# Tokens times Wq^T Wk as seven products of half-size blocks, from the second batch on

## The chip, the cores and the metric

The kernel runs on one core of a Trainium2 chip. The metric is the device time of one execution in microseconds. TensorE is called PE here (its weight loads PEld), VectorE DVE, ScalarE ACT, GpSimd POOL, and SyncE, whose queue issues most DMAs, SP.

## The reference

Eight batches of 256 tokens x 1024 features (x) and 256 context rows x 1024 (ctx_4096) go through a gated cross attention and a gated feed-forward block. Cut to what matters:

```python
xn = _layernorm(x)
Q = einsum('btx,dx->btd', xn, Wq) + bq          # 1024 x 1024
K = einsum('bpx,dx->bpd', ctx, Wk) + bk
attn = softmax(einsum('btd,bpd->btp', Q, K) / sqrt(1024))
x = x + tanh(g_xattn) * einsum('btp,bpd->btd', attn, ctx)
# feed-forward, 1024 -> 2752 -> 1024; each linear layer quantises its input rows
# and its weight rows to 8-bit steps (max-abs / 127) before the product
h = silu(qlinear(xn2, w_gate)) * qlinear(xn2, w_up)
x = x + tanh(g_ffn) * qlinear(h, w_down)
```

All inputs and the output are float32.

## The kernel before

The kernel has three parts. The first (to about 107 us) forms the map M = Wq^T Wk, 1024 x 1024 in f32, kept in SBUF as `mt` [128, 8, 1024], by seven products of half-size blocks. The bias of the queries becomes a column vector `u_col`. The second part, the attention half (about 107 to 455 us), runs over the eight batches. The third is the feed-forward part in bf16 (about 460 us to the end), whose weights stream through a ring of four buffers `wring` (tag `wp`, 8 KB per partition each), loaded by SP from the quantised copies in DRAM.

In the attention half the tokens of a batch lie transposed in `xT` [128, 8 feature chunks, 256 tokens], and `H` [128, 8, 256] is M^T applied to them plus `u_col`. `queries_product(j)` makes chunk j of H: eight matmuls of a 128 x 128 block of `mt` with 256 columns of `xT`, summed in a PSUM bank (tags g and s), and one ACT operation that adds the bias and writes H. `scores` multiplies H with the transposed features `fT` into two PSUM banks, one for each tile of 128 tokens; the eight matmuls of a tile read chunks 0 to 7 of H in order.

The order of every engine is the order of the program (`manual_schedule`). For batch b the program is: `softmax_stage(b)` (scores of tile 0, transposes of two quarters of the next batch's tokens into xT, half of the scores of tile 1, the other two quarters, the rest), then blocks 0 to 7 of the *next* batch's H through `queries_between(j)`, with work of this batch between them: `attend` after blocks 1 and 2 (attention times features), `residual` on DVE after each, statistics and normalisation of tokens on DVE, transposes of the next features (`features_transposed`, copied by ACT) after blocks 2 to 5, and `steps` on DVE (normalise, row maximum, scale to quantisation steps) for the two token tiles. `store_steps` rounds them on ACT and stores them.

Between all this `prepare()` advances the quantisation of the feed-forward weights by one piece: SP loads `raw`, DVE takes the row maximum (L126), POOL scales (L220 for w_gate and w_up, L232 for w_down), ACT rounds to bf16 (L257, L245), and SP transposes and stores. Load, DVE and POOL, ACT, and store belong to different pieces in one call: piece i is loaded, piece i-2 gets its maximum and scaling, piece i-3 is rounded. Four `raw` buffers go round. In batches 0 to 4 `queries_between` calls it from block 2 on, in batches 5 and 6 from block 1 on.

In batch 6 the first four weight buffers of the feed-forward part are loaded (`load_weights` at blocks 1, 3, 5 and 7).

Of the kernel before, what the change touches and what calls it, by code (L numbers as in the profile page):

```python
# [9 lines left out]
F32 = mybir.dt.float32  # L10
BF16 = mybir.dt.bfloat16
AF = mybir.ActivationFunctionType
ALU = mybir.AluOpType
# [4 lines left out]
P = 128  # L18
# [9 lines left out]
def gated_xattn_ffn_kernel(  # L28
# [26 lines left out]
    nc = tc.nc  # L55
    B, S, D = x.shape
# [3 lines left out]
    NTT = S // P  # L60
# [5 lines left out]
    HB = 512  # L66
# [8 lines left out]
    small = ctx.enter_context(tc.tile_pool(name="small", bufs=2))  # L75
# [29 lines left out]
    def store_as_rows(dst, cols, tag, pool):  # L105

        n = cols.shape[1]
        pt = bank(tag)
        nc.tensor.transpose(pt[:n, :P], cols, ident)
        rows = pool.tile([n, P], F32, name="rows", tag="rows", bufs=2)  # L110
        nc.scalar.copy(rows, pt[:n, :P])
        nc.gpsimd.dma_start(out=dst, in_=rows)
# [50 lines left out]
    def bank(tag):  # L163

        return psum.tile([P, HB], F32, name="ps_" + tag, tag=tag)
# [8 lines left out]
    if True:  # L174
        wraw = keep_scope.enter_context(tc.tile_pool(name="wraw", bufs=4, side=right))
        wkeep = keep_scope.enter_context(tc.tile_pool(name="wkeep", bufs=1, side=right))
        mt = wkeep.tile([P, KC, D], F32, name="mt")
        u_col = wkeep.tile([P, KC], F32, name="u_col")
# [88 lines left out]
        def prepare_keep(i):  # L267
            src, kind, part, r = pieces[i]
            if i in turned:
                slot = r % 2 if kind == "wgT" or rows_of(r) < P else r % 2 + 2  # L270
                nc.sync.dma_start(out=w_dram[r // 2][:, slot], in_=turned.pop(i))

        def prepare(n=1):
            for _ in range(n):
                i = step[0]
                if 0 <= i - 5 < len(pieces):
                    prepare_keep(i - 5)
                if i < len(pieces):
                    prepare_load(i)
                if 0 <= i - 3 < len(pieces):  # L280
                    prepare_store(i - 3)
                if 0 <= i - 2 < len(pieces):
                    prepare_scale(i - 2)
                step[0] += 1
# [9 lines left out]
        KH = KC // 2  # L294
# [3 lines left out]
        xT = f_right.tile([P, KC, NTT * P], F32, name="xT", tag="xT")  # L298
# [98 lines left out]
        for k in range(KH):  # L397
            pm = bank("g" if k < 2 else "tr")
# [43 lines left out]
        def transposes(src, blocks):  # L442
            pt = bank("tr").rearrange("p (i t) -> p i t", t=P)
            for i, k in enumerate(blocks):
                nc.tensor.transpose(pt[:, i, :], src[:, k * P : (k + 1) * P], ident)  # L445
            return pt
# [17 lines left out]
        def quarter_transposed(dst, src, g, copy):  # L464

            t, ks = g // 2, range(g % 2 * 4, g % 2 * 4 + 4)
            pt = transposes(src[t], ks)
            copy(dst[:, ks.start : ks.stop, t * P : (t + 1) * P], pt)  # L468
# [12 lines left out]
        stats = Rows()  # L481
# [41 lines left out]
        wring = ctx.enter_context(tc.tile_pool(name="wring", bufs=4, reuse_waits="tile"))  # L523
        weights, loads = [], [p for b in range(B) for p in range(NPR)]

        def load_weights():
# [11 lines left out]
        f_left = work_scope.enter_context(  # L538
            tc.tile_pool(name="f_left", bufs=1, reuse_waits="tile")
        )  # L540
        H = work.tile([P, KC, NTT * P], F32, name="H", bufs=1)
        fT = work.tile([P, KC, L], F32, name="fT", bufs=1)

        def queries_product(j):

            ph = bank("s" if j in (2, 4, 6) else "g")[:, : NTT * P]
            for k in range(KC):
                nc.tensor.matmul(  # L548
                    ph, lhsT=mt[:, k, j * P : (j + 1) * P], rhs=xT[:, k, :],
                    start=(k == 0), stop=(k == KC - 1),  # L550
                )
            nc.scalar.activation(H[:, j, :], ph, AF.Identity, bias=u_col[:, j : j + 1])

        def features_transposed(b, g, copy):
            quarter_transposed(fT, [f_tiles[b][:, l, :] for l in range(NLT)], g, copy)
# [8 lines left out]
        def scores(ps, t, js):  # L564
            for j in js:
                nc.tensor.matmul(  # L566
                    ps[:, :L], lhsT=H[:, j, t * P : (t + 1) * P], rhs=fT[:, j, :],
                    start=(j == 0), stop=(j == KC - 1),
# [51 lines left out]
        def steps(i, xr, stats):  # L620
            normalise(xr, xr, stats, i % NTT)
            scaled(i, xr, nc.vector)
            return xr
# [21 lines left out]
        stats = Rows()  # L645
        for j in range(KC):
            queries_product(j)
            prepare()
            if j == 2:
                for t in range(NTT):  # L650
                    stats.sums(t, xn[t])
            if j == 3:
                stats.root()
                stats.inverse()
            if j in (4, 5):
                normalise(xn[j - 4], xn[j - 4], stats, j - 4)
            if j == 3:
                load_features(1, f_left)
            if j in (2, 3, 4, 5):
                features_transposed(0, j - 2, nc.scalar.copy)  # L660

        def softmax_stage(b, xn):

            nxt = b + 1 < B
            pss = [bank("s") for _ in range(NTT)]
            scores(pss[0], 0, range(KC))
            if nxt:
                quarter_transposed(xT, xn, 0, nc.scalar.copy)
                quarter_transposed(xT, xn, 1, nc.scalar.copy)
            nums = [numerators(pss[0], shift(pss[0], cq[b][:, 0:1]))]  # L670
            scores(pss[1], 1, range(KC // 2))
            if nxt:
                quarter_transposed(xT, xn, 2, nc.scalar.copy)
                quarter_transposed(xT, xn, 3, nc.scalar.copy)
                prepare()
            scores(pss[1], 1, range(KC // 2, KC))
            nums.append(numerators(pss[1], shift(pss[1], cq[b][:, 1:2])))
            return nums

        def queries_between(j):  # L680
            queries_product(j)
            if j > (0 if b > B - 4 else 1):
                prepare()
            if b == B - 2 and j % 2:
                load_weights()

        waiting = None
        for b in range(B - 1):
            nxt = b + 2 < B
            nums = softmax_stage(b, xn)  # L690
            tokens_bias(b + 1, xn, scratch)
            if waiting:
                store_steps(*waiting)
            queries_between(0)
            xr = load_tokens(b, "xr")
            if nxt:
                xn = load_tokens(b + 2, "xn")
            pT = numerators_transposed(nums[0][0])
            prepare()
            queries_between(1)  # L700
            pas = attend(b, pT)
            pT = numerators_transposed(nums[1][0])
            residual(b * NTT, pas, xr[0], nums[0][1])
            nc.gpsimd.dma_start(out=x2_dram[b * NTT], in_=xr[0])
            if nxt:
                stats = Rows()
                for t in range(NTT):
                    stats.sums(t, xn[t])
                stats.root()
            prepare()  # L710
            queries_between(2)
            if nxt:
                stats.inverse()
                for t in range(NTT):
                    normalise(xn[t], xn[t], stats, t)
            features_transposed(b + 1, 0, nc.scalar.copy)
            pas = attend(b, pT)
            residual(b * NTT + 1, pas, xr[1], nums[1][1])
            nc.gpsimd.dma_start(out=x2_dram[b * NTT + 1], in_=xr[1])
            stats = Rows()  # L720
            stats.sums(0, xr[0])
            prepare()
            queries_between(3)
            stats.sums(1, xr[1])
            stats.root()
            if nxt:
                load_features(b + 2, (f_right, f_left)[b % 2])
            features_transposed(b + 1, 1, nc.scalar.copy)
            queries_between(4)
            stats.inverse()  # L730
            y = steps(b * NTT, xr[0], stats)
            features_transposed(b + 1, 2, nc.scalar.copy)
            queries_between(5)
            store_steps(b * NTT, y)
            features_transposed(b + 1, 3, nc.scalar.copy)
            if b == B - 2:
                store_as_rows(sx_dram[: b * NTT, :], sx_all[:, : b * NTT], "tr", work)
            queries_between(6)
            y = steps(b * NTT + 1, xr[1], stats)
            queries_between(7)  # L740
            waiting = (b * NTT + 1, y)
        assert step[0] >= len(pieces) + 3 and not turned
        keep_scope.close()
# [242 lines left out]
    first = {"xq": tokens_in, "sx": sx01[:, 0:1, :], "h": [], "tag": "s"}  # L986
# [6 lines left out]
    xr = load_tokens(B - 1, "xr")  # L993
# [11 lines left out]
    stats = Rows()  # L1005
# [6 lines left out]
    y = {}  # L1012
# [161 lines left out]
    b = B - 1  # L1174
# [52 lines left out]
    t, half = key = ALL[3]  # L1227
    for i in range(2):
        cols = slice(i * HB // 2, (i + 1) * HB // 2)
# [45 lines left out]
```

## Time and profile before

| | |
|---|---|
| time, median of 3 runs | 917.39 us (917.38 to 917.77) |
| profiled execution: span from first to last instruction | 914.9 us |
| its instructions | 14767 |
| granted TensorE clock, mean | 0.999 |
| PE busy | 906.3 us (99%) |
| DVE, ACT, POOL busy | 658.3, 466.6, 329.2 us |
| matmul groups of L548 (queries): busy | 144.6 us (bank tag g), 86.9 us (tag s) |
| matmul groups of L566 (scores), L595 (attend) | 58.9, 57.6 us |

The profile gives the span of one execution; the time of a run is measured around it, 2.5 us more at the median. In a line of the groups stand line, engine, operation, tiles and shape, count, busy time, mean duration of one, and the idle time just before with what ended it. In a line of the timeline stand start, duration, engine, line, operation, tiles and count, and in brackets the idle time before it and its releaser. One f32 matmul leaves two records on PE and two weight loads on PEld.

### The profile page before, as it was taken

Reading aid. Unit: us, or ns where it says so; the run is one execution under the profiler, and the core shown is the slowest. Engines: PE = TensorE matmul, PEld = TensorE weight load, DVE = VectorE, ACT = ScalarE, POOL = GpSimd, SP = SyncE. Lnnn points to the kernel's source line nnn. Section 1 sums busy time; section 2 is a strip of 40 time slices with the busy share of each in tenths; the row PEclk is TensorE's granted clock in tenths of the full one; section 3 lists DMA queues with packets and bytes.
Section 4 is the critical chain, followed back from the end, with each engine's and each line's share of the span. In section 5 each row is a group of like instructions: output and inputs, shape, how many; then the busy total and the mean of one; then the engine's idle time right before and its main releaser. Section 6 shows DMA issues by size and latency. Waiting matters only on the chain.

```text
span 914.9 us, 14767 instructions
## 1 busy us (share of the span) xinstructions
PE 906.3 (99%) x5379; PEld 681.3 (74%) x5394; DVE 658.3 (72%) x1328; ACT 466.6 (51%) x812; POOL 329.2 (36%) x444
## 2 busy tenths in 40 slices
PE   9999999999999999999999999999999999999997
PEld 5444588888887878787878886858778586876854
DVE  5888845958585858685678888676676766767677
ACT  0123334454545444544438688466484755748450
POOL 0034211212121212121112367639194582928621
PEclk9999999999999999999999999999999999999999
DMA  9359988789888889997779995977959597784821
GB/s 329 131 147 329 288 192 243 223 229 259 244 245 248 239 221 256 252 259 225 245 230 307 355 346 161 331 205 272 308 187 335 165 320 241 249 321 140 288 69 69
DMA packets 137848, 221.98 MB, mean 243 GB/s; under 512 B 92056, under 2 KB 93360, under 8 KB 127536
## 3 DMA queue, kind: packets, MB, share of 16 engines
q1 hardware_dynamic: 125872, 189.82, 69.0%
q0 software_dynamic: 6720, 22.56, 6.6%
q10 hardware_dynamic: 5184, 8.66, 2.6%
q8 instruction: 42, 0.69, 0.3%
q14 instruction: 30, 0.25, 0.1%
HBM read 167.52 MB, written 32.26 MB: 218 GB/s over the span
## 4 chain that ended last, share of the span: by engine, by line
PE 94%; DVE 4%; DMA 1%; issue 0%; ACT 0%; DVEq 0%; SPq 0%
PE ps_g L788 17%; PE ps_tr L788 16%; PE ps_g L548 14%; PE ps_s L548 8%; PE ps_s L948 7%; PE ps_s L566 6%; PE ps_a L595 5%; PE ps_a L948 5%; PE ps_s L342 4%; PE ps_tr L445 3%; PE ps_a L342 3%; PE ps_tr L342 2%; PE ps_g L342 2%; PE ps_g L1182 1%; DMA xn<-in_x_dram 1%; PE ps_tr L1182 1%
## 5 line engine op out<-in xcount | busy, mean ns | idle before, releaser
L788 PEld LDWEIGHTS <-wp 128*128 128x128 bf16 x2752 | 269.2, 98 | 33.0 <-issue 0.6
L788 PE MATMUL ps_g<-xqb,wp 128*128 128x256 bf16 x1408 | 168.1, 273 | 0.0
L788 PE MATMUL ps_tr<-xqb,wp 128*128 128x256 bf16 x1344 | 161.1, 273 | 0.0
L220 POOL TENSOR_SCALAR raw<-raw,inv 128x1024 f32<-128x1024 f32 (+1 forms) x44 | 56.3, 1280 | 247.5 <-DVE inv L122 140.1
L548 PE MATMUL ps_g<-xT,mt 128*128 128x256 f32 x640 | 144.6, 379 | 0.2 <-ACT xT L468 0.2
L548 PEld LDWEIGHTS ps_g<-xT,mt 128*128 128x128 f32 x640 | 120.3, 190 | 19.1 <-issue 3.3
L800 ACT ACTIVATE g<-g,swg 128x256 f32<-128x256 f32 (+1 forms) x176 | 79.6, 498 | 55.1 <-DVE g L798 54.9
L798 DVE TENSOR_TENSOR g<-ps_g,sx 128x512 f32<-128x512 f32 x88 | 60.7, 690 | 54.3 <-PE ps_g L788 54.1
L813 DVE SCALAR_TENSOR_TENSOR h<-ps_tr,swu,g 128x256 f32<-128x256 f32 x168 | 74.0, 480 | 35.8 <-PE ps_tr L788 25.5
L548 PE MATMUL ps_s<-xT,mt 128*128 128x256 f32 x384 | 86.9, 379 | 0.0
L257 ACT ACTIVATE rq<-raw,nmagic 128x1024 bf16<-128x1024 f32 (+1 forms) x44 | 50.6, 1149 | 59.4 <-POOL raw L220 52.7
L976 POOL TENSOR_TENSOR c<-c,swd_bc 128x512 f32<-128x512 f32 x26 | 33.0, 1271 | 130.6 <-issue 122.0
L548 PEld LDWEIGHTS ps_s<-xT,mt 128*128 128x128 f32 x384 | 71.2, 190 | 8.7
L948 PEld LDWEIGHTS <-gs 128*128 128x128 bf16 x385 | 37.6, 98 | 42.3
L821 ACT ACTIVATE ps_a<-h 128x512 f32<-128x512 f32 (+2 forms) x77 | 43.0, 558 | 51.3 <-DVE h L813 51.3
L566 PE MATMUL ps_s<-fT,H 128*128 128x256 f32 x256 | 58.9, 379 | 0.0
L927 POOL TENSOR_TENSOR gs<-hq 128x256 bf16<-128x256 bf16 x77 | 51.4, 668 | 18.3 <-ACT hq L887 18.0
L595 PE MATMUL ps_a<-fn,pT 128*128 128x512 f32 x128 | 57.6, 592 | 0.0
L886 ACT ACTIVATE h<-h,magic 128x512 f32<-128x512 f32 x82 | 55.5, 708 | 3.9 <-DVE h L879 3.8
L126 DVE TENSOR_REDUCE wam<-raw 128x1 f32<-128x1024 f32 (+1 forms) x44 | 53.3, 1210 | 4.1 <-DMA raw<-in_L_ffn_w_gate_dram 4.0
L887 ACT ACTIVATE hq<-h,nmagic 128x512 bf16<-128x512 f32 x82 | 55.5, 709 | 0.5
L566 PEld LDWEIGHTS ps_s<-fT,H 128*128 128x128 f32 x256 | 47.5, 190 | 5.9
(195 smaller groups left out, 1353.7 us busy)
## 6 DMA issues: line engine op xcount, KB each, us to landing
wp<-w_dram SPq DMA_DIRECT2D x80, 1024.0 KB, 6.6
w_dram<-wt SPq DMA_DIRECT2D x43, 256.0 KB, 4.1
raw<-in_L_ffn_w_gate_dram SPq DMA_DIRECT2D x21, 512.0 KB, 4.8
raw<-in_L_ffn_w_up_dram SPq DMA_DIRECT2D x21, 512.0 KB, 4.7
fn<-in_ctx_dram SPq DMA_DIRECT2D x8, 1024.0 KB, 6.9
raw<-in_L_ffn_w_down_dram SPq DMA_DIRECT2D x16, 512.0 KB, 7.1
xr<-in_x_dram SPq DMA_DIRECT2D x16, 512.0 KB, 4.2
x_dram<-xr POOLq DMA_DIRECT2D x16, 512.0 KB, 5.0
```

The source lines that it names most:

```text
L220: nc.gpsimd.tensor_scalar(raw[:n], raw[:n], inv, MAGIC, ALU.mult, ALU.add)
L342: nc.tensor.matmul(pm, lhsT=a[:, c, k * P : (k + 1) * P], rhs=b[:, c, :], start=start, stop=stop)
L548: nc.tensor.matmul(ph, lhsT=mt[:, k, j * P : (j + 1) * P], rhs=xT[:, k, :], start=(k == 0), stop=(k == KC - 1),)
L566: nc.tensor.matmul(ps[:, :L], lhsT=H[:, j, t * P : (t + 1) * P], rhs=fT[:, j, :], start=(j == 0), stop=(j == KC - 1),)
L595: nc.tensor.matmul(pas[h], lhsT=pT[:, l, :], rhs=f_tiles[b][:, l, halves[h]], start=(l == 0), stop=(l == NLT - 1),)
L788: nc.tensor.matmul(banks[slot // 2][:, slot % 2, :], lhsT=w[:, slot, k, :], rhs=block["xq"][:, k, :], start=(k == 0), stop=(k == KC - 1),)
L798: nc.vector.tensor_tensor(g, pg, block["sx"].to_broadcast((P, 2, TB)), ALU.mult)
L800: nc.scalar.activation(g[:n, i, :], g[:n, i, :], AF.Silu, scale=swg[:n, c : c + 1])
L813: nc.vector.scalar_tensor_tensor(h[:n, i, :], src, swu[:n, c : c + 1], g[:n, i, :], ALU.mult, ALU.mult)
L886: nc.scalar.activation(h, h, AF.Identity, bias=magic)
L887: nc.scalar.activation(hq, h, AF.Identity, bias=nmagic)
L948: nc.tensor.matmul(pm[:, cols], lhsT=a, rhs=w, start=(p == 0), stop=(p == NPR - 1))
```

## The change

From the second batch on, H is made of seven products of half-size blocks (Strassen's scheme in Winograd's form) instead of eight blocks of chunks. M is cut into four blocks `m11` to `m22` of 512 x 512, the tokens into four blocks of 512 features x 128 tokens, H likewise.

- The sums of the map's blocks, `ms1`, `ms2` and `ms4`, take three of the four buffers of the weight ring, and the three token sums `xsum` the fourth, until the feed-forward part loads its weights there; `ms3` is written over `m21` after the first batch's queries. POOL makes them (`map_sums`, 16 operations, emitted during the first batch's blocks).
- Per batch POOL makes four token sums (`token_sums`, in `softmax_stage` after the last quarter of xT is copied); one of them overwrites a block of xT.
- `half_product` is 16 matmuls of 128 x 128 blocks with 128 columns. Products 1 and 2 follow each other in one PSUM bank, product 5 and the product of `ms4` in another. `evicted_half` writes a result with its bias in four ACT operations of 128 columns; `combined_half` adds results to H on DVE, five operations of 128 x 512 per batch.
- There are seven `queries_between` per batch; `prepare()` is called from block 1 on in every batch, and the DVE steps of the second token tile come before block 6. DVE's sums of a block come after its `prepare()`. `load_weights` in batch 6 is called at blocks 1, 3, 5 and 6.

```diff
+        m11, m21 = mt[:, :KH, :HB], mt[:, :KH, HB:]
+        m12, m22 = mt[:, KH:, :HB], mt[:, KH:, HB:]
+        ms1, ms2, ms4 = (
+            wring.tile([P, KH, HB], F32, name=f"ms{i}", tag="wp") for i in (1, 2, 4)
+        )
+        xsum = wring.tile([P, 3, KH, P], F32, name="xsum", tag="wp")
+        ms3 = m21
...
+        def map_sums(dst, a, b, op):
+            for k in range(KH):
+                nc.gpsimd.tensor_tensor(dst[:, k, :], a[:, k, :], b[:, k, :], op)
+
+        u_step = small.tile([P, KH], F32, name="u_step")
+        nc.vector.tensor_tensor(u_step, u_col[:, KH:], u_col[:, :KH], ALU.subtract)
...
+        def token_sums():
+            for dst, a, b in (
+                (xs1, x12, x11), (xs2, x22, xs1), (xs3, x22, x12), (xs4, xs2, x21)
+            ):
+                nc.gpsimd.tensor_tensor(dst, a, b, ALU.subtract)
+
+        def half_product(a, b, pm=None, tag=None):
+
+            first = pm is None
+            if first:
+                pm = bank(tag).rearrange("p (i t) -> p i t", t=P)
+            for i in range(KH):
+                for k in range(KH):
+                    nc.tensor.matmul(
+                        pm[:, i, :], lhsT=a[:, k, i * P : (i + 1) * P], rhs=b[:, k, :],
+                        start=(first and i == k == 0), stop=(i == k == KH - 1),
+                        skip_group_check=not first,
+                    )
+            return pm
+
+        def evicted_half(dst, pm, cols):
+            for i in range(KH):
+                nc.scalar.activation(
+                    dst[:, i, :], pm[:, i, :], AF.Identity, bias=cols[:, i : i + 1]
+                )
+
+        def combined_half(dst, x, y, op=ALU.add):
+            nc.vector.tensor_tensor(dst, x, y, op)
...
+        def queries_part(j):
+
+            if j == 0:
+                part[1] = half_product(m11, x11, tag="g")
+                evicted_half(h12, part[1], u_col[:, :KH])
+            elif j == 1:
+                part[5] = half_product(ms1, xs1, tag="g")
+                nc.scalar.copy(h22, part[5])
+            elif j == 2:
+                half_product(m12, x21, part[1])
+                evicted_half(h11, part[1], u_col[:, :KH])
+            elif j == 3:
+                part[6] = half_product(ms2, xs2, tag="s")
+            elif j == 4:
+                part[7] = half_product(ms3, xs3, tag="s")
+                evicted_half(h21, part[7], u_step)
+            elif j == 5:
+                half_product(ms4, x22, part[5])
+            else:
+                part[4] = half_product(m22, xs4, tag="g")
+
+        def queries_sums(j):
+
+            if j == 3:
+                combined_half(h12, h12, part[6])
+            elif j == 4:
+                combined_half(h21, h21, h12)
+                combined_half(h22, h22, h21)
+            elif j == 5:
+                combined_half(h12, h12, part[5])
+            elif j == 6:
+                combined_half(h21, h21, part[4], ALU.subtract)
...
             queries_product(j)
+            if j == 1:
+                map_sums(ms1, m21, m22, ALU.add)
+            elif j == 3:
+                map_sums(ms2, ms1, m11, ALU.subtract)
+            elif j == 5:
+                map_sums(ms4, m12, ms2, ALU.subtract)
+            elif j == 7:
+                map_sums(ms3, m11, m21, ALU.subtract)
             prepare()
...
                 quarter_transposed(xT, xn, 3, nc.scalar.copy)
+                token_sums()
                 prepare()
...
         def queries_between(j):
-            queries_product(j)
-            if j > (0 if b > B - 4 else 1):
+            queries_part(j)
+            if j > 0:
                 prepare()
-            if b == B - 2 and j % 2:
+            queries_sums(j)
+            if b == B - 2 and j in (1, 3, 5, 6):
                 load_weights()
...
+            y = steps(b * NTT + 1, xr[1], stats)
             queries_between(6)
-            y = steps(b * NTT + 1, xr[1], stats)
-            queries_between(7)
             waiting = (b * NTT + 1, y)
```

More of the change, by code (lines that the diff above doesn't have):

```diff
@@ L552, in queries_product @@
             nc.scalar.activation(H[:, j, :], ph, AF.Identity, bias=u_col[:, j : j + 1])
+        def map_sums(dst, a, b, op):
[3 more added lines that the diff above has]
+        nc.vector.tensor_tensor(u_step, u_col[:, KH:], u_col[:, :KH], ALU.subtract)
+        (x11, x12), (x21, x22) = [
+            [xT[:, i * KH : (i + 1) * KH, t * P : (t + 1) * P] for t in range(NTT)]
+            for i in range(2)
+        ]
@@ new lines, in gated_xattn_ffn_kernel @@
+        (h11, h12), (h21, h22) = [
+            [H[:, i * KH : (i + 1) * KH, t * P : (t + 1) * P] for t in range(NTT)]
+            for i in range(2)
+        ]
+        xs1, xs2, xs4 = (xsum[:, i] for i in range(3))
+        xs3 = x12
+        def token_sums():
[15 more added lines that the diff above has]
+            return pm
@@ new lines, in evicted_half @@
+        def evicted_half(dst, pm, cols):
[5 more added lines that the diff above has]
+            nc.vector.tensor_tensor(dst, x, y, op)
+        part = {}
+        def queries_part(j):
[17 more added lines that the diff above has]
+                part[4] = half_product(m22, xs4, tag="g")
```

## The prediction

> **What bounds the kernel now.** I read the busy table first, then the chain that ended last, then the costliest groups.
>
> ```profile
> PE 906.3 (99%) x5379; PEld 681.3 (74%) x5394; DVE 658.3 (72%) x1328; ACT 466.6 (51%) x812; POOL 329.2 (36%) x444
> ...
> PE 94%; DVE 4%; DMA 1%; issue 0%; ACT 0%; DVEq 0%; SPq 0%
> ...
> L548 PE MATMUL ps_g<-xT,mt 128*128 128x256 f32 x640 | 144.6, 379 | 0.2 <-ACT xT L468 0.2
> L548 PEld LDWEIGHTS ps_g<-xT,mt 128*128 128x128 f32 x640 | 120.3, 190 | 19.1 <-issue 3.3
> ```
>
> PE is the bound by a wide margin, and the line that the change attacks, L548 (640 records here, 384 more into the other bank tag), has no idle time. One f32 matmul leaves two records. DVE at 72% is an average; what it has left inside one batch of the attention half decides this case, so I read the timeline of one batch. I take batch 5 (S = 363.76 to 409.11, 45.35 us; S is the start of its scores), because in it the weight preparation already steps after query block 1, as the changed kernel does in every batch.
>
> ```profile
> 363.76 3.62 PE L566 MATMUL ps_s<-fT,H 128*128 128x256 f32 x16
> 367.21 1.04 PE L445 MATMUL ps_tr<-ident,xn 128*128 128x128 f32 x8
> 368.09 1.89 PE L566 MATMUL ps_s<-fT,H 128*128 128x256 f32 x8
> ...
> 405.66 3.62 PE L548 MATMUL ps_g<-xT,mt 128*128 128x256 f32 x16
> 409.11 3.62 PE L566 MATMUL ps_s<-fT,H 128*128 128x256 f32 x16
> ```
>
> PE has no hole. Start to start, 16 records of 256 columns take 3.45 us (0.216 each); eight transposes, one f32 weight load and one pass of 128 columns each, take 0.88 (0.110 each). VectorE in the same batch, from the first residual on:
>
> ```profile
> 383.18 0.75 DVE L606 SCALAR_TENSOR_TENSOR xr<-ps_a,r,xr 128x512 f32<-128x512 f32 x1 [0.97 <-PE ps_a L595]
> ...
> 389.88 1.22 DVE L126 TENSOR_REDUCE dam<-raw 128x1 f32<-128x1024 f32 x1 [1.79 <-DMA raw<-in_L_ffn_w_down_dram]
> ...
> 399.57 0.94 DVE L143 TENSOR_SCALAR v<-mv 128x2 f32<-128x2 f32 x1
> 400.79 0.17 DVE L151 RECIPROCAL rr<-rt 128x2 f32<-128x2 f32 x1 [0.27 <-ACT rt L146]
> ...
> 405.68 1.22 DVE L126 TENSOR_REDUCE wam<-raw 128x1 f32<-128x1024 f32 x1 [0.41 <-DMA raw<-in_L_ffn_w_gate_dram]
> ...
> 410.48 1.21 DVE L126 TENSOR_REDUCE wam<-raw 128x1 f32<-128x1024 f32 x1
> ...
> 411.92 0.16 DVE L122 RECIPROCAL inv<-swu 128x1 f32<-128x1 f32 x1
> 412.76 0.42 DVE L574 TENSOR_REDUCE nm<-ps_s 128x1 f32<-128x256 f32 x1 [0.68 <-PE ps_s L566]
> ```
>
> From 383.18 on it has no slack but the waits shown, and it finishes its batch at 412.08, 3 us after PE has begun the next one. That harms nobody before, since ScalarE writes all of H.
>
> **PE, the part removed.** Eight blocks of 16 records at 0.216 (27.6 us) become seven blocks of 32 records with 128 columns. Price of such a record: 0.110 by the transposes; by the bias columns, where only weight loads bind, (0.86 - 0.19) / 6 = 0.112:
>
> ```profile
> 76.75 0.86 PEld L452 LDWEIGHTS ps_tr<-ones,xT 128*128 128x128 f32 x7 [0.24 <-issue]
> ```
>
> I take 0.110: 224 x 0.110 = 24.6, so 3.0 us less per batch (2.5 by the other row), 21 over seven batches. The 190 ns in the group table is the latency of one load, not its spacing. With PE alone the kernel would come to about 896.
>
> **VectorE, the part added.** Five sums of 128x512 per batch, at 0.62 start to start and 0.70 for the last (rows of the same form: 0.68 to 0.69 long): 3.2 us. They stand in VectorE's program order, and the last one, lower half of H for the first token tile minus product 4, stands behind both quantisation steps and one weight maximum. The fifth score matmul of the next batch reads it. This is the new wait; behind it on PE is everything.
>
> When is it done? Template: VectorE ends at 412.08, or S + 48.3. The changed kernel has one weight maximum fewer in this tail; with its wait it takes 405.27 to 407.27: -2.0. The sums: +3.2. The pair of sums at step 4 needs product 7, which ScalarE evicts in four pieces behind the square root and a copy of fT:
>
> ```profile
> 400.55 0.20 ACT L146 ACTIVATE rt<-v 128x2 f32<-128x2 f32 x1 [5.90 <-DVE v L143]
> 400.66 0.57 ACT L468 COPY fT<-ps_tr 128x512 f32<-128x512 f32 x1
> 401.13 0.48 ACT L552 ACTIVATE H<-ps_s,u_col 128x256 f32<-128x256 f32 x1
> ```
>
> So the evictions start 0.6 us after v ends, and four at about 0.27 (256 columns take 0.37 start to start; estimated for half) with the latency of the last take 1.3 to 1.4: VectorE waits about 2.0 where it waited 0.3, +1.7. Sum: S + 51.2. PE could take the fifth score matmul at 45.35 - 3.0 + 1.73 = S + 44.1. It waits 7.1 us, and the period becomes 51.2 - 1.73 = 49.5, which is 4.1 more than now. The stall repeats: the next first residual follows the scores by the same PE work.
>
> Lower bound: without the 1.79 wait for the second w_down tile (batches 0 to 3 show none, in another order) and with the evictions free, 46.0. Upper: later SP loads and sums, 51.
>
> **PE's clock.** A hole of 7 us is new. The trace shows the clock after PE's end (last matmul ended about 910.1); in this line of the windows view five engines are idle and the next number is the granted clock:
>
> ```profile
> 912.60:914.90 2.30, 0.00 (x0) 0.00 (x0) 0.00 (x0) 0.00 (x0) 0.00 (x0) 0.50 0.00 0
> ```
>
> It is halved some 2.5 us after the last matmul. At the start, 16 records of the new products' own shape (L366, from 1.07) took 3.74 us, 0.21 apart instead of 0.11, so half speed ended near 4.6. By these rows each stall is followed by up to 3.5 us at half speed, in the scores, which are in the loop: +1.8, lower end 0, upper 2.6. I take 1.8.
>
> [...]
>
> **POOL.** Four token sums of 128x512: 1.27 each by L976's row, 5.1 per batch, from about S + 8 when the last xT copy ends; the first is needed at S + 12.4, so PE is covered by 3 us. Behind them wait three weight scalings, then ScalarE's roundings, then SP's transposes and the w_down load of the template: 0 to +1. Beside them VectorE multiplies tokens by v; v at 399.57 took 0.94 instead of 0.17 while POOL ran, so VectorE may lose up to 1.2 before its residual, where it has about 1.9 of slack. I take 0.3 for both.
>
> [...]
>
> The 16 map sums (20.3 us) lie in batch 0's query stage, where POOL works 6.4 of 30 us; ScalarE's first w_down rounding there stands at 129.87 and its scaling can be done by 124: 0 to +3, taken 0.5.
>
> **The rest.** ScalarE: 8 x 0.37 becomes 12 x 0.27 + 0.58, 0.9 more, hidden except in the chain above. Weight loads of the ring now wait for products 5, 6, ms4 and 4 on SP; behind the fourth waits xqb, which before landed at 461.17 for a use at 461.69. PE's stall gives that the time back: 0, up to +2. In the last of the seven batches nothing is normalised (5.4 us of VectorE less), so its stall is about 2.5: period 44.6, -0.8.
>
> Sum: period 49.5 + 1.8 + 0.3 = 51.6, +6.25, six times: +37.5; -0.8; +0.5. The span of 914.9 becomes 952.1; with the 2.5 that the median 917.39 lies above that span, 954.6; I say 954.
>
> **Rivals.** (1) As summed, but the clock holds or recovers at once: 954 - 11 = 943. For it: it is granted in full wherever PE works after 4.6. (2) VectorE is late by less (no DMA wait, quick evictions, short hole): periods of 46.0 to 48.0 give +3 to +15, 919 to 933. For it: batches 0 to 3 wait for no w_down tile. (3) Faster: the last sum is ready by S + 44.1, so PE's 21 us stand, 896. It decides if VectorE's tail is 7.1 us shorter than summed; against it, even without waits the tail ends at S + 47.7. (4) Weight loads don't overlap passes of 128 columns: 190 ns a record, 224 x 0.19 = 42.6, +15 a batch, 1020; against it both rows at 0.11.
>
> **Numbers.** Forecast 0.47, (1) 0.24, (2) 0.18, (3) 0.06, (4) 0.03, something near no change 0.02. The 8-in-10 range drops (3), (4) and the lower part of (2): 925 to 966; the upper end is a period 2 us longer. A measurement tells 0.2% (1.8 us) from no change: faster 0.06, same 0.01, slower 0.93.
>
> **What would show it.** Right: L591 records 0.11 apart; a PE wait of about 7 us per batch at the score matmul, released by VectorE's L605; VectorE without idle from first residual to last sum but at the w_down tile and the evictions; a granted clock under 1 in the batches; PE's busy share down. Wrong: no wait at the scores, or the period below 45; then VectorE's tail was mis-summed. If records stand 0.19 apart, (4) holds.

## The result, and the profile after

| | before | changed |
|---|---|---|
| time, median | 917.58 us (917.38 to 918.49, 4 runs) | 959.47 us (955.99 to 962.47, 4 runs) |
| profiled execution: its time; its span | 914.9 us span | 962.47 us; 960.7 us span |
| ratio, 95% interval | | 1.0454 (1.0427 to 1.048) |

The changed kernel is slower by 4.5%. In its page I look at the busy line, the granted clock, the chain that ended last, and the groups of the scores (L654) and of the half-size products (L591).

```profile
PE 906.8 (94%) x6051; PEld 698.8 (73%) x6066; DVE 693.5 (72%) x1364; ACT 468.9 (49%) x847; POOL 398.0 (41%) x488
...
PEclk9999999999898979898999999999999999999999
...
PE 66%; DVE 19%; DMA 7%; ACT 4%; issue 2%; SPq 1%; ACTq 0%; DVEq 0%
...
L654 PE MATMUL ps_s<-fT,H 128*128 128x256 f32 x256 | 71.3, 430 | 39.9 <-DVE H L605 39.9
...
L591 PE MATMUL ps_g<-xT,mt 128*128 128x128 f32 x448 | 52.3, 275 | 0.0
```

PE's busy time is the same as before, in a span 46 us longer, so the smaller products' gain was eaten up inside the busy time as well as beside it: the scores run at half clock for a while (the dips in the clock line; 0.50 granted from 290.58 to 297.40 us, for one), and PE is idle for 39.9 us ahead of them. PE's share of the chain falls from 94% to 66%; DVE has 19% of it. The waits view gives the times and the longest of each (total, count, longest):

```profile
PE ps_s L654 <- DVE H L605: 39.9, 7, 7.2
...
DVE dam L126 <- DMA raw<-in_L_ffn_w_down_dram: 19.0, 8, 2.8
...
DVE H L605 <- ACT H L600: 12.5, 7, 1.8
...
PE ps_a L683 <- ACT pT L676: 2.3, 6, 0.5
...
PE ps_g L885 <- DMA xqb<-xq_dram: 1.6, 1, 1.6
```

There are seven waits at the scores, one for each batch with a last sum. One of them follows in PE's timeline, and then VectorE's way to it, from the start of the scores at 284.95 on (PE's view ends behind 346.75; the fifth to eighth score matmul leave eight records):

```profile
334.09 3.74 PE L591 MATMUL ps_g<-xsum,mt 128*128 128x128 f32 x32
337.66 1.89 PE L654 MATMUL ps_s<-fT,H 128*128 128x256 f32 x8
346.75 1.62 PE L654 MATMUL ps_s<-fT,H 128*128 128x256 f32 x3 [7.19 <-DVE H L605]
```

```profile
304.01 1.21 DVE L473 SCALAR_TENSOR_TENSOR prod<-xn,v_bc 128x1024 bf16<-128x1024 f32 x1
...
305.27 2.17 DVE L473 SCALAR_TENSOR_TENSOR prod<-xn,v_bc 128x1024 bf16<-128x1024 f32 x1
...
307.48 1.11 DVE L477 TENSOR_SCALAR cq<-cq,bqbk 128x2 f32<-128x2 f32 x1
...
322.19 1.22 DVE L126 TENSOR_REDUCE dam<-raw 128x1 f32<-128x1024 f32 x1 [2.79 <-DMA raw<-in_L_ffn_w_down_dram]
...
334.61 1.42 DVE L605 TENSOR_TENSOR H<-H 128x512 f32<-128x512 f32 x2 [1.78 <-ACT H L600]
...
344.35 1.21 DVE L126 TENSOR_REDUCE wam<-raw 128x1 f32<-128x1024 f32 x1
...
345.93 0.67 DVE L605 TENSOR_TENSOR H<-H,ps_g 128x512 f32<-128x512 f32 x1
```

The last sum (345.93) is VectorE's last piece of the batch, behind both quantisation steps and one weight maximum, and PE resumes 0.15 us after it ends. POOL's token sums in the same stretch; alone such a sum takes 1.27:

```profile
302.81 1.27 POOL L582 TENSOR_TENSOR xsum<-xT,xsum 128x512 f32<-128x512 f32 x1
304.04 2.32 POOL L582 TENSOR_TENSOR xT<-xT 128x512 f32<-128x512 f32 x1
306.32 2.25 POOL L582 TENSOR_TENSOR xsum<-xsum,xT 128x512 f32<-128x512 f32 x1
```

From start of scores to start of scores the periods are 42.72, 50.10, 53.18, 52.71, 53.44, 52.17 and 53.27 us, where the kernel before has 45.35 to 45.72. The first has no hole (no idle stretch of PE) yet, so 42.72 is PE's own work. The six others average 52.48, which is made of:

| per period, mean of six | us |
|---|---|
| PE's work at full clock | 42.72 |
| hole at the fifth score matmul (4.04 to 7.19) | 6.35 |
| other PE waits, mostly for the transposed numerators (L683) | 0.48 |
| lost at half clock (half of the time that PE works in the half-speed stretches) | 2.32 |
| not attributed (records beside a hole or a change of clock) | 0.61 |

The span is 45.76 us longer: 39.67 from the seven periods, 1.78 from a shorter hole at the last scores, 1.61 from a wait for the quantised tokens (`xqb`) at the first gate product, 2.31 from before the first scores (see the last section), 0.39 not followed up. The profile is that of the longest of the four runs (962.47 us); the medians are 41.9 us apart.

### The profile page after: what moved, and what is told of

Its sections match the earlier page's. It is cut to its first block, busy times and chain, and to the rows that moved or that the text cites. A ratio compares the mean times of both kernels' runs of the same rounds, so it can differ in the third digit from the quotient of the medians.

```text
span 960.7 us, 16240 instructions
## 1 busy us (share of the span) xinstructions
PE 906.8 (94%) x6051; PEld 698.8 (73%) x6066; DVE 693.5 (72%) x1364; ACT 468.9 (49%) x847; POOL 398.0 (41%) x488
## 4 chain that ended last, share of the span: by engine, by line
PE 66%; DVE 19%; DMA 7%; ACT 4%; issue 2%; SPq 1%; ACTq 0%; DVEq 0%
PE ps_g L885 16%; PE ps_tr L885 15%; PE ps_s L1045 6%; PE ps_s L654 5%; PE ps_a L1045 5%; DMA raw<-in_L_ffn_w_down_dram 4%; PE ps_s L342 2%; PE ps_a L683 2%; DVE H L605 2%; DVE prod L473 2%; PE ps_tr L445 2%; DVE st L140 2%; PE ps_g L555 2%; PE ps_a L342 2%; DVE xam L126 2%
## 5 line engine op out<-in xcount | busy, mean ns | idle before, releaser
L654 PE MATMUL ps_s<-fT,H 128*128 128x256 f32 x256 | 71.3, 430 | 39.9 <-DVE H L605 39.9
L654 PEld LDWEIGHTS ps_s<-fT,H 128*128 128x128 f32 x256 | 53.3, 218 | 50.0 <-issue 42.5
L257 ACT ACTIVATE rq<-raw,nmagic 128x1024 bf16<-128x1024 f32 (+1 forms) x44 | 51.0, 1160 | 62.0 <-POOL raw L220 50.1
L683 PE MATMUL ps_a<-fn,pT 128*128 128x512 f32 x128 | 58.2, 597 | 2.3 <-ACT pT L676 2.3
L1024 POOL TENSOR_TENSOR gs<-hq 128x256 bf16<-128x256 bf16 x77 | 51.3, 667 | 18.3 <-ACT hq L984 18.0
L591 PE MATMUL ps_g<-xT,mt 128*128 128x128 f32 x448 | 52.3, 275 | 0.0
L591 PEld LDWEIGHTS ps_g<-xT,mt 128*128 128x128 f32 x448 | 51.7, 192 | 0.4
L1028 POOL TENSOR_TENSOR gs<-hq 128x256 bf16<-128x256 bf16 x77 | 51.6, 670 | 0.0
L929 DVE TENSOR_TENSOR acc<-acc,ps_a 128x512 f32<-128x512 f32 (+2 forms) x77 | 47.9, 630 | 4.9 <-ACT ps_a L918 4.0
```

The costliest lines, as they stand in the source:

```text
L591: nc.tensor.matmul(pm[:, i, :], lhsT=a[:, k, i * P : (i + 1) * P], rhs=b[:, k, :], start=(first and i == k == 0), stop=(i == k == KH - 1), ...
L654: nc.tensor.matmul(ps[:, :L], lhsT=H[:, j, t * P : (t + 1) * P], rhs=fT[:, j, :], start=(j == 0), stop=(j == KC - 1),)
L683: nc.tensor.matmul(pas[h], lhsT=pT[:, l, :], rhs=f_tiles[b][:, l, halves[h]], start=(l == 0), stop=(l == NLT - 1),)
```

## The experiments

The theory: the last sum stands late in VectorE's order, the hole lets the granted clock fall, and the two together cost more than the products save. All kernels below are edits of the changed kernel, except the last one.

**1. Without the last sum, and with another order.**

```diff
# no_last_sum
-            elif j == 6:
-                combined_half(h21, h21, part[4], ALU.subtract)
```

> Leaves out the last sum of each batch (lower half of H for token tile 0 minus product 4), so that the scores wait for no sum behind the quantisation steps. Theory A (PE waits for that sum, which stands at the end of VectorE's tail, and pays for the hole in clock as well): the holes of about 7 us at the score matmul go, the granted clock is back at 1.0, and the time falls from 959 to 900-917 us; the upper end if VectorE's tail, which is as long as before, now runs into the next batch's row maximum. Theory B (products of 128 columns or the extra work on POOL and ScalarE cost the time themselves): one sum of 0.7 us less per batch, 955 us or more.

```diff
# sums_first
             queries_part(j)
+            queries_sums(j)
             if j > 0:
                 prepare()
-            queries_sums(j)
...
-            y = steps(b * NTT + 1, xr[1], stats)
             queries_between(6)
+            y = steps(b * NTT + 1, xr[1], stats)
```

> Same work, other order: VectorE's sums stand ahead of the weight maximum of their block, and the second tile's quantisation steps (3.2 us) come after the last sum. Theory A: 3.2 + 1.6 us fewer ahead of the last sum, so the hole shrinks from about 7 to about 2 us and most of the clock loss (2.4 us per batch) goes with it: a period of 45-47 us instead of 53, 915-928 us in all. Theory B (records, POOL, ScalarE): order of VectorE's work does not matter, 955 us or more.

Measured: 932.29 us without the sum (ratio 1.0165, 1.0137 to 1.0192) and 932.44 with the sums first (1.0158, 1.0141 to 1.0174). The two agree, so the last sum's place, not the sum, costs 27 us. Both times lie above what theory A gave: at five of the scores a hole of 2.3 to 2.9 us is left (in no_last_sum one of the five is 1.05), and in both kernels it is ScalarE's copy that ends it. In sums_first, PE and then ACT:

```profile
277.00 3.45 PE L654 MATMUL ps_s<-fT,H 128*128 128x256 f32 x8 [2.94 <-ACT fT L468]
```

```profile
274.80 1.15 ACT L725 ACTIVATE xq<-xr,nmagic 128x1024 bf16<-128x1024 f32 x1 [3.15 <-DVE xr L704]
...
276.36 0.58 ACT L468 COPY fT<-ps_tr 128x512 f32<-128x512 f32 x1 [0.41 <-ACT xq L725]
```

The last quarter of the transposed features, which the fifth score matmul also reads, is copied behind a rounding that waits 3.15 us for VectorE's first quantisation step. The second wait had been hidden behind the first.

**2. The clock by itself.** Thirteen matmuls that no one reads fill the hole.

```diff
# filler
-            scores(pss[0], 0, range(KC))
+            scores(pss[0], 0, range(KC // 2))
+            if b:
+                spare = [bank("a") for _ in range(2)]
+                for i in range(13 if b > 1 else 8):
+                    nc.tensor.matmul(
+                        spare[0][:, :L], lhsT=ident, rhs=fT[:, 0, :], start=True, stop=True)
+            scores(pss[0], 0, range(KC // 2, KC))
```

> Thirteen matmuls of 256 columns (5.6 us; eight in the first of the batches) whose result nobody reads are put into the hole, between the fourth and the fifth score matmul. If the clock gate costs what the trace suggests (3.7 to 5.8 us at half speed after each hole, so 2.4 us each): granted clock 1.0, period down by about 2.4 us, 945 us (941 to 950). If the clock is no part of it: 959 us. If the hole were not idle time of PE: about 990 us.

Measured: 948.78 us (1.0338, 1.0316 to 1.036), with a page whose clock line shows no dip:

```profile
PEclk9999999999999999999999999999999999999999
```

The periods after the first average 49.86 instead of 52.48: 2.6 us of a hole's price is the clock, as the 2.32 of the account above says by another way. Profile against profile the span is 14.4 us shorter: 15.7 from the six periods and 1.4 ahead of the first scores, less 1.3 for a longer wait for `xqb` at the first gate product (2.9 instead of 1.6 us) and about 1.6 for the one half-speed stretch that is left, right behind that wait. The medians are only 10.7 us apart, as the changed kernel's profile is that of its longest run.

**3. VectorE's wait for the weight tile.** The next tokens' normalisation goes ahead of block 2, so that the second w_down tile is asked for later.

```diff
# norm_first
             prepare()
-            queries_between(2)
             if nxt:
                 stats.inverse()
                 for t in range(NTT):
                     normalise(xn[t], xn[t], stats, t)
+            queries_between(2)
```

> VectorE's inverse root and normalisation of the next tokens (2.4 us) are put ahead of the maximum of the second w_down tile, for whose load it waits 1.8 to 2.8 us. Theory A: the wait is hidden by them, 2 to 2.5 us less in five or six periods, 945 to 950 us. Rival: the wait for the load only moves, or something else on the chain ends as late, 956 us or more.

Measured: 952.33 us (1.0383, 1.0365 to 1.0401), 7 us less, between theory A and its rival. The wait for the second tile, 2.3 to 2.8 us in five periods, falls to at most 0.4 (in the fifth VectorE then waits 1.7 us for the third tile), and the holes fall to 4.1 to 6.5. The periods after the first average 51.06, 1.4 us less; why not the 2 to 2.5 expected was not followed up.

**4. POOL's sums out of the softmax's stage.**

```diff
# late_token_sums
-                token_sums()
+                token_sums(slice(0, 1))
...
             nc.gpsimd.dma_start(out=x2_dram[b * NTT], in_=xr[0])
+            token_sums(slice(1, 4))
```

> The change with one edit: GpSimd's sums of three of the four pairs of token halves are issued after the first residual and not in the softmax's stage. The computation is unchanged. Theory A (the two engines slow each other in the softmax's stage by about 1.9 us on VectorE, which delays the quantised tokens, the load of the second w_down tile behind them, and so the last sum): the load lands about 1.5 us earlier, the hole is 4 to 5.5 us, and the time 945 to 954 us. Rival (the slowing there is covered, as VectorE waits for the tile in any case): the time stays at 956 to 962 us.

Measured: 954.11 us (1.0398, 1.038 to 1.0417), 5 us less, just outside what theory A gave (945 to 954). VectorE's timeline, with the scores from 283.23 on:

```profile
303.03 1.22 DVE L473 SCALAR_TENSOR_TENSOR prod<-xn,v_bc 128x1024 bf16<-128x1024 f32 x1
...
315.14 1.82 DVE L143 TENSOR_SCALAR v<-mv 128x2 f32<-128x2 f32 x1
...
319.03 1.22 DVE L126 TENSOR_REDUCE dam<-raw 128x1 f32<-128x1024 f32 x1 [0.94 <-DMA raw<-in_L_ffn_w_down_dram]
```

The multiplication takes 1.22 instead of 2.17, and the tile's maximum starts 35.80 us after the scores instead of 37.24, 1.44 earlier. The slowing moves to `v` (1.82 instead of 0.17), where the wait for the tile covers it (0.94 of that wait is still left). But the hole stays at 5.7 to 7.1 us, not the 4 to 5.5 expected: PE loses its other waits too (0.48 becomes 0), and so arrives at the hole earlier. The hole is the difference of two ways through the batch; the period is what shows a gain in one of them (51.40 instead of 52.48).

**5. What comes after the last sum.** copy_first is sums_first with ScalarE's copy ahead of the first quantisation; copy_late adds the late token sums; two kernels then add one edit each.

```diff
# copy_first
-            store_steps(b * NTT, y)
             features_transposed(b + 1, 3, nc.scalar.copy)
+            store_steps(b * NTT, y)
# copy_late: copy_first and late_token_sums
# copy_late_root: copy_late, and queries_between(j, then) calls then() after queries_part(j)
-            stats.root()
...
-            queries_between(4)
+            queries_between(4, stats.root)
# copy_late_norm: copy_late and norm_first
```

> The sums of a product stand ahead of the next operand's preparation, the second tile's quantisation steps behind block 6 (as in sums_first), and besides ScalarE copies the last quarter of the transposed features ahead of the first tile's quantisation, not behind it. The computation is unchanged. Theory A (in sums_first the hole of 2.9 us at the fifth score matmul is ScalarE's copy, which stood behind a quantisation that waits 3.15 us for VectorE): the copy no longer waits for that; what is late next is the last sum, which ended about 1 us earlier than the copy: a hole of 0 to 2.0 us, periods of 44 to 47.5 us, a time of 911 to 928 us; if the granted clock falls after a hole of that size the upper half, if not the lower. Theory B (the copy is late because the last of product 7's evictions and the root stand ahead of it on ScalarE): the hole stays at 2.5 to 3 us and the time at 929 to 934 us.

> copy_first, and besides GpSimd's sums of three of the four pairs of token halves after the first residual (as in late_token_sums). The computation is unchanged. It tells how much of the way from copy_first (926 us) to all_late_tokens (901 us) is the slowing of VectorE by GpSimd alone, with the next tokens' normalisation, the root and the weight ring's fourth load left where the change has them. Theory A (the load of the second w_down tile, late through that slowing, is what makes the last sum late): the hole of 2.0 us at the fifth score matmul falls to 0 to 0.7 us, periods of 42.9 to 44.5 us, 903 to 915 us. Theory B (the normalisation ahead of the queries' preparation and the root ahead of the evictions are the rest of it): the hole stays at 1.2 us or more, and the time at 918 to 926 us.

> copy_late, and besides ScalarE's square root of the second tile's statistics stands behind block 4's evictions and product 7's, not ahead of them. The computation is unchanged. Of the two edits that stand between copy_late (920 us, holes of 2 us) and all_late_tokens (901 us, none) this is the one by itself. Theory A (the first of the last two sums waits 1.78 us for product 7's evictions, which stand behind a root that waits for VectorE's variance; that wait is what is left of the hole): the hole falls to 0 to 0.5 us and the time to 904 to 911 us. Rival (VectorE is late by its work in any case, which the normalisation ahead of block 2 would bring forward): the hole stays at 1 us or more, and the time at 914 to 921 us.

> copy_late, and besides the next tokens' inverse and normalisation stand ahead of block 2's preparation on VectorE. The computation is unchanged. The other of the two edits by itself. Theory A (the wait for product 7's evictions behind the root is what is left of the hole): the root's input comes no earlier, the hole stays at 1 us or more and the time at 914 to 921 us. Rival (VectorE's order is what is left: with the normalisation earlier, the second weight tile has landed when it is asked for, the variance and with it the root come earlier too): a hole of 0 to 0.7 us and a time of 904 to 912 us.

| kernel | time, us | ratio (95%) | holes at the fifth score matmul, us |
|---|---|---|---|
| copy_first | 925.94 | 1.0096 (1.0064 to 1.0128) | 1.8 to 2.0 |
| copy_late | 920.34 | 1.0044 (1.0022 to 1.0065) | 0.9 to 2.0 |
| copy_late_root | 913.09 | 0.9952 (0.9934 to 0.9969) | 0 to 1.3 |
| copy_late_norm | 913.90 | 0.9961 (0.994 to 0.9981) | 0.9 to 1.8 |

The holes are those of one profiled execution each, copy_first's the shortest of its six runs (920.53 us) and copy_late's the longest of its eight (925.95), so between these two rows the medians tell more than the holes. copy_first bears out theory A: ScalarE's copy was next, and the last sum is late again after it. In copy_late theory A of that expectation fell, with holes up to 2.0 us: the late token sums shorten the wait for the second tile (2.1 to 2.8 us in five batches of copy_first, 0.8 to 1.5 in four of the same five batches of copy_late) but are not all of the rest. Another part stands in its ACT and DVE timelines:

```profile
268.52 0.20 ACT L146 ACTIVATE rt<-v 128x2 f32<-128x2 f32 x1 [8.93 <-DVE v L143]
...
269.10 1.14 ACT L600 ACTIVATE H<-ps_s,u_step 128x128 f32<-128x128 f32 x4
```

```profile
270.28 1.42 DVE L605 TENSOR_TENSOR H<-H 128x512 f32<-128x512 f32 x2 [1.78 <-ACT H L600]
```

ScalarE idles 8.93 us at a root that waits for VectorE's variance, product 7 has been lying in PSUM behind it, and VectorE then waits 1.78 for its eviction: two engines wait for each other in turn. With the root behind the evictions that wait is gone in all but one batch, and 7.2 us of the time with it; holes of up to 1.3 us are left where I expected at most 0.5, and the time is 2 us above my 904 to 911: `xqb` now comes 3.6 us late at the first gate product, with half a clock behind it. The normalisation alone brings about as much, 6.4 us, with the 1.78 still there in every batch; there VectorE waits for the second tile in only one of the five batches looked at above (0.8 us). Its holes of 0.9 to 1.8 us follow theory A of that expectation, and the time lies just below its lower edge (914), so neither theory is borne out alone. Both edits had a part in what was left.

**6. All orders together.** all_orders has sums_first, copy_first, norm_first and the root's place, and the weight ring's fourth load behind `xqb`; all_late_tokens adds the late token sums.

```diff
-            if b == B - 2 and j in (1, 3, 5, 6):
+            if b == B - 2 and j in (1, 3, 5):
...
     load_as_rows(sx01.rearrange("p b t -> p (b t)"), sx_dram[: 2 * NTT, :])
+    load_weights()
```

> All edits of order at once: the sums ahead of the preparation, the second tile's steps behind block 6, ScalarE's last copy of the features ahead of the first quantisation, its root behind the evictions of product 7, the next tokens' normalisation ahead of block 2, and the fourth load of the weight ring behind the quantised queries' load. The computation is unchanged. Theory A (TensorE's own work is 42.7 us a batch, which the first period of the change showed, and the rest of the 52.7 is holes and the clock that falls after them): no hole at the scores, periods of 42.7 to 43.3 us, a granted clock near 1.0, and a time of 899 to 908 us, below the kernel before. Theory B (another wait of 1 us or more takes the hole's place, and the clock falls behind it): periods of 45 to 48 us and a time of 915 to 932 us.

> As all_orders, and besides GpSimd's sums of three of the four pairs of token halves for the next batch are issued after the first residual and not in the softmax's stage. The computation is unchanged. Theory A (GpSimd's and VectorE's instructions slow each other where they run together, 1.2 to 2.2 us for the two, and the softmax's stage is where this delays the quantised tokens and the load of the second w_down tile): VectorE's multiplications of the queries' preparation take 1.2 us and not 2.2, and the time is 0 to 10 us below all_orders, the more the larger its hole is. Rival (the sums only move the slowing to another place, or come late for the products): the time is that of all_orders to 0.3%, or 5 to 15 us above it, with TensorE waiting for GpSimd at the products' first matmuls.

Measured: 905.97 us (0.9871, 0.985 to 0.9891) and 900.82 us (0.9819, 0.9798 to 0.984). The second is 16 us below the kernel before. Its page:

```profile
PE 890.7 (99%) x6066; PEld 688.4 (77%) x6066; DVE 694.1 (77%) x1364; ACT 469.3 (52%) x847; POOL 390.9 (43%) x488
...
PE 97%; DVE 2%; DMA 1%; issue 0%; ACT 0%; DVEq 0%
```

DVE has the same work as in the changed kernel (694.1 against 693.5), and PE does not wait for it at the scores. One batch end, PE and then DVE:

```profile
351.71 3.62 PE L654 MATMUL ps_s<-fT,H 128*128 128x256 f32 x16
```

```profile
351.73 1.28 DVE L605 TENSOR_TENSOR H<-H,ps_g 128x512 f32<-128x512 f32 x2
```

The last two sums run while PE does the first four score matmuls. The periods are 42.72 to 43.14. In all_orders the holes at the scores are gone too, but waits of 0.5 to 1.1 us remain at L683 (periods of 43.5 to 44.5); the late token sums remove them.

**7. The orders without the change.** Every one of these edits that the kernel before has a place for, on the kernel before.

> The kernel before, with the edits of order of all_orders that it has a place for: the next tokens' normalisation ahead of block 2, the root behind that block's evictions on ScalarE, the last copy of the features ahead of the first quantisation's store, and the weight ring's fourth load behind the quantised queries' load. The computation is unchanged. Theory A (TensorE has no hole of 0.4 us in the seven batches of the kernel before, so there is nothing for another order to fill, and what all_late_tokens gains on the kernel before is the products' smaller work): 914 to 919 us, within 0.3% of the kernel before. Rival (the orders shorten the batches by themselves, by waits that the profile puts under other names): below 912 us, and a part of the gain of 16 us is not the change's.

Measured: 916.97 us, ratio 0.9995 (0.9986 to 1.0004), the same. Its periods are 45.35 and 45.46. So the orders gain nothing by themselves: the 16 us are the half-size products', and the orders only let them through.

## Why the prediction was right, and where its terms were off

Forecast 954.0, measured 959.47, in the range. The forecast sum added 37.2 us to the span; the medians differ by 41.9, the profiled spans by 45.76. By its own steps:

- **PE's price.** A group of 32 records of 128 columns spans 3.73 us, its last one 0.27: (3.73 - 0.27) / 31 = 0.112 each. That is the row of the bias columns, where the weight loads stand 0.112 apart too; I had taken the transposes' 0.110. 2.63 us a batch were saved, not 3.0. Rival (4), 0.19 a record, is excluded.
- **The wait.** Right in place, releaser and size: 7.1 forecast, 6.8 to 7.2 in four of the six full batches, 6.35 in the mean. That the size came so near is partly luck: the tile, 1.0 later than summed, lengthens the hole, and PE's smaller saving (0.37) and the shorter wait for the evictions (0.2) take a part of that back.
- **Its terms.** Evictions 1.78 (2.0 summed). The w_down tile 2.79, where I had carried over 1.79. The difference is the POOL term that I sized at 0.3: two VectorE operations lose 0.95 and 0.88 beside the token sums. My cover for that, 1.9 us of slack ahead of the residual, is there (0.56 us of waiting is still left ahead of it), but the loss goes another way: by ScalarE's rounding of the tokens, which waited for `prod`, SP's queue and the tile. Experiment 4 prices it at 1.1 us a period. My 0.3 was too small: these two operations alone lost 1.8 us, and the rows agree with engines that wait for each other by turns (last section).
- **The clock.** 1.8 a stall forecast, 2.32 in the account, 2.6 by experiment 2. I had taken up to 3.5 us at half speed for a stall; the stretches lasted 3.4, 6.8 or 10.2 us, a part of them inside the hole. No row stands behind the upper end of 2.6. Rival (1), a clock that holds, would have given 943; with the clock held by filler the time is 948.8.
- **The last of the seven batches.** A stall of 2.5 forecast, 1.78 measured.
- **Tile, evictions and clock together:** 51.6 + 1.0 - 0.2 + 0.5 = 52.9 for a period; the last five average 52.95. This was added up after the result and is no test of the terms.
- **Map sums, ring.** 0.5 forecast, nothing measured: the start of the scores is explained without them (last section). The wait for `xqb`, 0 forecast with up to 2, was 1.61.
- **Rival (2), VectorE late by less.** Periods of 46 to 48 occur in none of the changed kernel's batches with a hole; the smallest is 50.1, behind the first hole of 4.04, before the stall has carried over from batch to batch.
- **Rival (3), faster.** I said that VectorE's tail would have to be 7.1 us shorter. Its work did not have to be: the experiments show that most of the tail needn't stand ahead of the last sum. The 896 that I gave for PE alone is 899 with its measured price (917.4 - 7 x 2.63), and 900.8 was reached.

## What to carry to other kernels

A transform that saves products on the busiest engine moves sums into the order of others; place the result that the next stage reads first at the earliest point at which its inputs exist, ahead of work that nobody waits for. Removing the late instruction alone gave 27 of 59 us, since ScalarE's copy, a root that waits across engines, GpSimd's sums beside VectorE's work, and the next stage's load each came next: follow the chain again after each edit. And price a hole on TensorE with the clock that it costs, here 2.3 to 2.6 us on top of 6.

## What the runs showed of the hardware that I had not expected

**The clock changed on a grid.** In every profile here all changes of the granted clock lie a multiple of 3.413 us apart; in the changed kernel's batches the stretches at half speed last 3.41, 6.83 or 10.24 us, those at full speed between them 44.37. What went with a change was not the length of a hole but how much of one such window of 3.413 us was idle. Two holes of the same length, 2.03 and 2.04 us; the columns are the stretch, its length, the busy time (and count) of PE, PEld, DVE, ACT and POOL, the granted clock, the DMA share and GB/s. In copy_first the grid cuts the hole, which began at 272.01:

```profile
272.41:275.83 3.42, 1.79 (x8) 1.58 (x9) 3.28 (x7) 2.17 (x3) 0.19 (x1) 1.00 1.06 297
275.83:279.24 3.41, 3.41 (x25) 3.14 (x24) 3.17 (x7) 2.36 (x3) 1.36 (x1) 1.00 1.00 151
```

In copy_late the whole hole lies in one window, and the next one was granted half:

```profile
229.60:233.04 3.44, 1.40 (x7) 1.25 (x7) 3.30 (x6) 2.17 (x3) 0.00 (x0) 1.00 1.08 314
233.04:236.45 3.41, 3.41 (x13) 2.96 (x13) 3.20 (x7) 1.14 (x2) 1.54 (x1) 0.50 0.75 171
```

The 82 holes of 0.9 us or more in the 12 profiles of the changed kernel and its edits touch 139 windows: the 36 full-speed windows with 2.04 us or more idle were each followed by a half-speed one, the 76 with 1.94 or less by none. In the changed kernel's own profile the six windows at its large holes that were followed by half speed had 2.22 to 3.41 us idle, and no other full-speed window before PE's end had more than 1.62. At half speed, 19 windows with 0.99 or more idle were followed by another, 8 with 0.65 or less by full speed. That was read from the runs afterwards; no run was made to test it. The hole of 4.04 us, the shortest of the changed kernel's large ones, was followed by half speed too (0.50 from 188.18 to 191.59 us), and in copy_late one of 2.04 was enough.

**The grid's phase moved the time of a run.** The first half-speed stretch ended at 4.63 us in the profile of before and at 7.27 in that of the changed kernel. Half of the difference is 1.32; the other 0.99 of the 2.31 us at the start of the scores goes with a hole of 1.23 us at 99.1, in the map's part, whose cause I did not follow up. In the eight edits without such a hole (all but no_last_sum, sums_first and copy_late) the start of the scores is 136.64 plus half the difference of that end to 4.63, within 0.02 us, so POOL's 16 map sums cost nothing there. Runs of one kernel differ by more than this: copy_first's six go from 920.53 us at a mean granted clock of 0.999 to 931.06 at 0.992. That would fit holes of 2 us that the grid cuts in some runs and not in others, but only the first was profiled.

**Two engines held each other up, by turns.** A POOL token sum and a VectorE multiplication take 1.27 and 1.22 us alone, and up to 2.32 and 2.17 where they run together. The rows above read as waiting for the other to finish rather than as both running slower. The multiplication that began at 304.01, just ahead of a sum, kept its 1.21 us; the sum that began 0.03 us later ended 1.14 us after it; and the next multiplication ended 1.08 us after that sum. VectorE's `v` of two columns takes 0.17 alone and 1.82 beside such sums (at 315.14 in late_token_sums).
